# Order of the three passes in split products, and a norm handed over before a mixer, in a two-layer kernel on one core

## The chip, the cores and the metric

The kernel runs on one core of a Trainium2 chip. The metric is the device time of one execution in microseconds; lower is better. The core has five engines with a queue each: TensorE (PE in the profile), which multiplies and transposes, VectorE (DVE), ScalarE (ACT), GpSimd (POOL) and SyncE (SP), which here issues nearly all DMA transfers.

## The reference

Four batches of 512 rows of 256 values pass through two layers. Each layer normalizes its input, computes a mixed part `s` and a gate `g`, and adds their product:

```
xn = layernorm(x)
s  = mix(xn)                      # layer 0: linear map, RMS norm, plus xn; layer 1: attention, plus xn
g  = silu(W2 · fwht(silu(W1·xn) * (W3·xn)))
x  = x + s * g
```

In layer 0 the recurrence starts from zero and runs one step, so its mix is one 256 x 256 matrix, followed by an RMS norm. `fwht` is a Walsh-Hadamard transform over the 1024 hidden values. In layer 1 the mix is a causal attention with one head over 512 positions. All is in 32-bit floating point.

## The kernel before

**Split products.** Nearly every operand is kept as two tensors of the type `fp32r`: `hi`, a cast made by ACT, and `lo`, the rest, made by DVE as source minus `hi` (`split`, line 59). A product `l · r` is then three passes that add up in one PSUM bank: hi·hi, hi·lo and lo·hi. `mm3` (line 80) issues them for a list of terms, as a rule two, for the two halves of the 256 input values: first hi·hi of all terms, then for each term `l[0]·r[1]` (upper part of the stationary operand, lower part of the moving one) and `l[1]·r[0]`. Those who call `mm3` are the gate and up products of layer 0 (line 510), the mixer (717), the folded matrices (208 and 235), and in the attention `tq` (782), `v` (791), `sc` (807) and `pv` (858). The products of the hidden values (`down`, lines 469 and 573) and the gate products of layer 1 (`ffn_s`, line 556) write their three passes out themselves.

**Layer 0.** `ffn` (line 461) goes through a batch in eight chunks `c` of 128 hidden values. For each it makes two products, `gu0` and `gu1`, of twelve passes in all, then on ACT the silu, on DVE the product `h`, and the split of `h` into `hh` and `hl`. `down` of a chunk runs one chunk later. The weights come in four quarters, two chunks each; `split_w13` (line 118) makes their two parts in batch 0. Beside the chunks runs a list of tasks, generators that `Beside` (line 872) steps through, a step or so per slot, two slots a chunk. For each batch the list is built in the loop at line 993: in batch 0 the preparation of weights, `mixer(0)` and `norm(0, 1)`; in the later ones the gate of the batch before (`gate_all`), `mixer(b)`, `norm(0, b + 1)`, and preparations for layer 1 (`prep_w2`, `prep_second`, `prep_s`).

`norm(0, b)` (line 426) makes DVE's statistics, POOL's power -0.5, DVE's scaling, eight transposes on PE, and the split of the transposed input `xT` (`xt` in the profile). `mixer(b)` (line 708) makes 24 products of 256 columns in two halves, copies them out (`osb`), squares and sums them on ACT, takes the power on POOL, scales `osb` and adds it to `xn` on DVE.

**What sets the order.** In layer 0 the order in which each engine's instructions stand is chosen when the kernel is built: a scheduler lays them out by its own model of time, from the dependencies and the order in which the code hands them over, with a few ties (`after`). In the queue of an engine that order is then fixed. From line 1065 on, in layer 1, the products are tied to each other in the order of the code. The tags of PSUM that matter here are `gu` (three banks, the gate and up products), `ms` (three, transposes, mixer and most others) and `dn` (two, the sums over the chunks).

Of the kernel before, what the change touches and what calls it, by code (L numbers as in the profile page):

```python
# [35 lines left out]
def kernel(ctx: ExitStack, tc: tile.TileContext, a: dict, out: bass.AP):  # L36
# [40 lines left out]
    def transpose(*args):  # L77
        return in_line(nc.tensor.transpose, *args)

    def mm3(o, terms):  # L80

        seq = [(l[0], r[0]) for l, r in terms]
        for l, r in terms:
            seq += [(l[0], r[1]), (l[1], r[0])]
        for n, (l, r) in enumerate(seq):
            ins = matmul(o, l, r, start=n == 0, stop=n == len(seq) - 1)
        return ins
# [128 lines left out]
    def sl(i):  # L216
        return slice(i * P, (i + 1) * P)
# [80 lines left out]
    ALLS = slice(0, S)  # L298
    ALLD = slice(0, D)
# [161 lines left out]
    def ffn(name, xT, w13, w2, slot, defer=1, spare=(), parts=1, behind=False, tail=()):  # L461

        w2h, w2l = w2
        dn, outs, firsts = [], [], {}

        def down(c, hh, hl, tiles=range(NT)):
            if not dn:  # L470
                dn.extend(psum(f"{name}dn{i}", [P, 2, D], tag="dn", bufs=2) for i in range(2))
                outs.extend(dn[t // 2][:, t % 2, :] for t in range(NT))
            for t in tiles:
                o = outs[t]
                for n, (l, r) in enumerate(((hh, w2h), (hh, w2l), (hl, w2h))):
                    first = c == 0 and n == 0
                    stop = c == NH - 1 and n == 2

                    def one(start):
                        return matmul(  # L480
                            o, l[:, sl(t)], r[:, c, :], start=start, stop=stop, skip_group_check=True
                        )

                    if first and t % 2 == 1:
                        with tc.issue_after(firsts[t // 2].ins):
                            ins = one(False)
                    elif first:
                        ins = firsts[t // 2] = one(True)  # L490
                    else:
                        ins = one(False)
            return ins

        queue, gates, late = [], [], []
        for c in range(NH):
            with after(gates[-2] if behind and c >= 2 else None):
                wh, wl = w13(c // 2)
            gu = []
            for j in range(2):  # L500

                o = psum(f"{name}gu{c}_{j}", [P, S], **(DN[0] if behind and c == 1 else GU))
                cols = slice((c % 2) * D + j * P, (c % 2) * D + (j + 1) * P)
                gu.append((o, cols))
            for half in range(parts if c == 0 else 1):
                n = S // (parts if c == 0 else 1)
                ts_ = slice(half * n, (half + 1) * n)
                if parts == 1 or c:
                    for o, cols in gu:
                        last_up = mm3(o[:, ts_], k_pairs((wh, wl), cols, xT, ts_))  # L510
                    continue

                for n, (w, x) in enumerate(((wh, xT[0]), (wl, xT[0]), (wh, xT[1]))):
                    for o, cols in gu:
                        for k in range(2):
                            last_up = matmul(
                                o[:, ts_], w[:, k, cols], x[:, k, ts_],
                                start=n + k == 0, stop=n + k == 3,
                            )
            gu = [o for o, _ in gu]  # L520
            h = hid(f"{name}h{c}")
            first["silu"] = nc.scalar.activation(h, gu[0], AF.Silu)
            gates.append(nc.vector.tensor_tensor(h, h, gu[1], ALU.mult))  # L523
            first["gate"] = gates[-1]
            if c < len(spare):
                hh, hl = spare[c]
            else:
                hh = hid(f"{name}hh{c}", F32R)
                hl = hid(f"{name}hl{c}", F32R)
            if c < len(spare):  # L530
                nc.scalar.copy(hh, h)
                late.append((hl, h, hh))
            else:
                split(h, hh, hl)
            for _ in range(2 if c >= NH - 2 else 0):
                if late:
                    lo_, h_, hi_ = late.pop(0)
                    with after(gates[-1]):
                        nc.vector.tensor_tensor(lo_, h_, hi_.bitcast(F32), ALU.subtract)
            queue.append((c, hh, hl))  # L540
            ups = last_up if behind else None
            with after(gates[-1] if behind else None), after(ups):
                slot(2 * c)
            if len(queue) > defer:
                down(*queue.pop(0))
            with after(gates[-1] if behind else None), after(ups):
                slot(2 * c + 1)
        line["fixed"] = bool(tail)
        line["last"] = last_up
        for what in tail:  # L550
            what()
        for q in queue:
            down(*q)
        return dn
# [153 lines left out]
    def mixer(b):  # L708

        xn, xT, m = xns[0, b], xTs[0, b], first["m"]  # L710
        osb = t4(f"osb{b}", [P, NT, D])
        r = small(f"ssr{b}")
        junk = t2(f"junk{b}", [P, D])
        for i in range(2):
            o = psum(f"o0_{b}_{i}", [P, 2, D])
            for j in range(2):
                mm3(o[:, j, :], k_pairs(xT, sl(2 * i + j), m, ALLD))
            nc.scalar.copy(osb[:, 2 * i : 2 * i + 2, :], o)
            for t in (2 * i, 2 * i + 1):
                nc.scalar.activation(junk, osb[:, t, :], AF.Square, accum_out=r[:, t : t + 1])  # L720
            yield
        nc.vector.tensor_scalar(r, r, 1.0 / D, RMS_EPS, ALU.mult, ALU.add)
        nc.gpsimd.tensor_tensor(r, r, mhalf, ALU.pow)
        for t in range(NT):
            nc.vector.scalar_tensor_tensor(
                osb[:, t, :], osb[:, t, :], r[:, t : t + 1], nwb, ALU.mult, ALU.mult
            )
        nc.vector.tensor_tensor(xn, xn, osb, ALU.add)
        yield

    class Attention:
# [45 lines left out]
        def tq(self, j):  # L777
            b = self.b
            if j == 0:
                self.tqs = t4(f"tqh{b}", [P, 2, S], F32R), t4(f"tql{b}", [P, 2, S], F32R)  # L780
            o = psum(f"tq{b}_{j}", [P, S])
            mm3(o, k_pairs(first["wqk"], sl(j), self.xg, ALLS))
            split(o, self.tqs[0][:, j, :], self.tqs[1][:, j, :])

        def v(self, i, j):
# [207 lines left out]
    for b in range(B):  # L993
        tasks = []
        if b == 0:
            prep = prep_first()
            next(prep)
            tasks.append((prep, 12))
        if b:
            tasks.append((call(gate_all, f"g0_{b - 1}", dn, xns[0, b - 1], xs[b - 1]), 1))  # L1000
        tasks.append((mixer(b), MIXER))
        if b + 1 < B:
            if b:
                load_x(b + 1)
            if b == 2:
                tasks.append((prep_s(0), 4))
            tasks.append((norm(0, b + 1), NORM))
        if b == 0:
            early = w2_tile("early0"), w2_tile("early1")
            spare = [  # L1010
                [early[i][:, 2 * c : 2 * c + 2, :].rearrange("p a d -> p (a d)") for i in range(2)]
                for c in range(NH // 2)
            ]
        if b == 1:
            raw2_1 = load_w2(1)
            w2_1 = w2_tiles(1)
            tasks.append((prep_w2(1, raw2_1, w2_1, t4), W2P))
            tasks.append((prep_second(), 5))
        if b == 2:
            tasks += [(prep_s(1), 4), (norm(1, 0), NORM), (prep_s(2), 4)]  # L1020
        if b == 3:
            atts = [Attention(0)]
            at = atts[0]
            parts = run(at.xt_half, 0), run(at.xt_half, 1), at.xt, at.scaled, at.split_sums
            tasks += [(call(f), 1) for f in parts]
            norms = {1: norm(1, 1)}
            tasks.append((prep_s(3), 4))
        bg = Beside(*tasks)
        if b == 0:
            dn = ffn("f0_0", xTs[0, 0], w13, w2, bg.slot, NH, spare, parts=2, behind=True)  # L1030
        else:
            tail = [run(atts[0].tq, j) for j in range(2)] if b + 1 == B else []
            dn = ffn(f"f0_{b}", xTs[0, b], w13, w2, bg.slot, tail=tail)
        bg.finish()
# [148 lines left out]
```

## Time and profile before

| what | us |
|---|---|
| median of 3 runs (lowest, highest) | 361.06 (361.01, 361.54) |
| the profiled execution | 361.18 |
| its span, first to last instruction | 359.4 |
| PE busy | 352.8 |
| DVE busy | 287.5 |
| ACT busy | 197.9 |
| POOL busy | 20.8 |

All lines of the profile come from one execution. A row of its timeline has the start, the time, the engine, the line of the kernel, the operation and what it writes and reads (output<-inputs), the shapes and the count; a bracket at its end tells how long the engine was idle before and what ended the wait. Numbers of buffers and of chunks are left out in such names, so `f_2hl` is the lower part of the hidden values of any chunk, and the number tells the batch. `PEld` is the loading of a product's stationary operand. Products are pipelined: a row's time overlaps the next one's, so the pace is read from the starts. A line of `L70` is that of the helper through which all products pass.

### The profile page before, as it was taken

How to read it: one execution, taken by the hardware profiler on the slowest of the kernel's cores; microseconds unless marked ns; L12 is line 12 of the kernel's file. 1: busy time of each engine (PE TensorE's matmuls, PEld its weight loads, DVE VectorE, ACT ScalarE, POOL GpSimd, SP SyncE). 2: the span in 40 equal slices, each digit the busy share in tenths (PEclk: the TensorE clock that was granted, in tenths of full speed). 3: DMA queues.
4: the chain of work that ended last, by engine and by line, in shares of the span. 5: the costliest groups of instructions: out<-in, count | busy, mean ns of one | idle time of the engine just before them, and what ended most of it. 6: DMA issues, size and time to landing. Idle time of an engine off the chain costs nothing.

```text
span 359.4 us, 6279 instructions
## 1 busy us (share of the span) xinstructions
PE 352.8 (98%) x2477; PEld 327.2 (91%) x2477; DVE 287.5 (80%) x597; ACT 197.9 (55%) x373; POOL 20.8 (6%) x22
## 2 busy tenths in 40 slices
PE   8999999999999999999999999999999999999995
PEld 6878988888988898888999999999999999999995
DVE  6899658998579938998987957989679897568646
ACT  4666156265463425664477655576555676556443
POOL 2000110300020110100100001100011000000000
PEclk9999999999999999999999999999999999999999
DMA  7935000301044317656256136652554645345401
GB/s 237 339 102 192 2 1 2 114 3 60 0 168 172 132 44 249 243 181 191 90 216 253 58 148 207 226 208 95 204 193 162 214 169 204 128 159 196 191 2 58
DMA packets 16285, 52.25 MB, mean 145 GB/s; under 512 B 1633, under 2 KB 7937, under 8 KB 16257
## 3 DMA queue, kind: packets, MB, share of 16 engines
q1 hardware_dynamic: 15968, 51.60, 40.6%
q8 instruction: 19, 0.31, 0.4%
q10 hardware_dynamic: 288, 0.26, 0.2%
q14 instruction: 10, 0.07, 0.1%
HBM read 42.40 MB, written 9.45 MB: 144 GB/s over the span
## 4 chain that ended last, share of the span: by engine, by line
PE 85%; DVE 12%; ACT 1%; DMA 1%; POOL 1%; issue 0%; DVEq 0%
PE f_0gu L70 6%; PE f_1gu L70 6%; PE f_2gu L70 6%; PE f_3gu L70 6%; PE f_3dn L70 6%; PE f_2dn L70 6%; PE f_0dn L70 5%; PE f_1dn L70 5%; PE pv L70 4%; PE o L70 3%; PE tq L70 3%; PE v L70 2%; PE sc L70 2%; PE w2ps L70 1%; PE pt L70 1%; DVE neg L814 1%
## 5 line engine op out<-in xcount | busy, mean ns | idle before, releaser
L70 PE MATMUL f_1gu<-xt,w 128*128 128x512 f32 x96 | 24.9, 396 | 0.3 <-ACT xt L61 0.3
L70 PE MATMUL f_3gu<-xt,w 128*128 128x512 f32 x96 | 25.0, 396 | 0.0
L70 PE MATMUL f_2gu<-xt,w 128*128 128x512 f32 x96 | 24.8, 395 | 0.0
L70 PE MATMUL f_0gu<-xt,w 128*128 128x512 f32 (+1 forms) x108 | 24.3, 378 | 0.0
L70 PEld LDWEIGHTS f_0gu<-xt,w 128*128 128x128 f32 x108 | 18.4, 188 | 4.6 <-issue 1.0
L70 PEld LDWEIGHTS f_1gu<-xt,w 128*128 128x128 f32 x96 | 17.0, 188 | 3.7 <-ACT xt L61 0.5
L70 PEld LDWEIGHTS f_2gu<-xt,w 128*128 128x128 f32 x96 | 17.0, 188 | 3.0
L70 PEld LDWEIGHTS f_3gu<-xt,w 128*128 128x128 f32 x96 | 17.0, 188 | 2.9
L61 ACT CAST f_2hh<-f_2h 128x512 fp32r<-128x512 f32 x16 | 9.9, 622 | 15.6 <-DVE f_2h L523 12.5
L70 PE MATMUL f_3dn<-w2l,f_3hh 128*128 128x256 f32 x64 | 17.7, 281 | 0.0
L70 PE MATMUL f_3dn<-w2h,f_3hh 128*128 128x256 f32 x64 | 17.7, 281 | 0.0
L70 PE MATMUL f_1dn<-w2l,f_1hh 128*128 128x256 f32 x64 | 17.7, 281 | 0.0
L70 PE MATMUL f_2dn<-w2h,f_2hh 128*128 128x256 f32 x64 | 17.7, 282 | 0.0
L70 PE MATMUL f_1dn<-w2h,f_1hh 128*128 128x256 f32 x64 | 17.6, 280 | 0.0
L70 PE MATMUL f_2dn<-w2l,f_2hh 128*128 128x256 f32 x64 | 17.6, 280 | 0.0
L70 PE MATMUL f_3dn<-w2h,f_3hl 128*128 128x256 f32 x64 | 17.0, 281 | 0.0
L70 PE MATMUL f_1dn<-w2h,f_1hl 128*128 128x256 f32 x64 | 17.0, 281 | 0.0
L70 PE MATMUL f_2dn<-w2h,f_2hl 128*128 128x256 f32 x64 | 16.7, 281 | 0.0
L61 ACT CAST f_3hh<-f_3h 128x512 fp32r<-128x512 f32 (+1 forms) x17 | 10.0, 595 | 10.1 <-DVE f_3h L523 6.0
L61 ACT CAST f_1hh<-f_1h 128x512 fp32r<-128x512 f32 x16 | 9.9, 622 | 9.7 <-DVE f_1h L523 6.6
L62 DVE TENSOR_TENSOR f_2hl<-f_2h,f_2hh 128x512 fp32r<-128x512 f32 x16 | 10.9, 680 | 3.9 <-ACT f_2hh L61 3.8
L70 PE MATMUL f_0dn<-w2h,f_0hl 128*128 128x256 f32 x48 | 13.7, 284 | 0.1
(487 smaller groups left out, 1146.1 us busy)
## 6 DMA issues: line engine op xcount, KB each, us to landing
sw<-s SPq DMA_DIRECT2D x32, 896.0 KB, 5.4
s<-sp SPq DMA_DIRECT2D x8, 512.0 KB, 4.0
s<-sp SPq DMA_DIRECT2D x8, 384.0 KB, 2.8
w2raw<-in_w SPq DMA_DIRECT2D x4, 512.0 KB, 5.1
sraw<-in_w SPq DMA_DIRECT2D x4, 512.0 KB, 3.3
mrb<-there SPq DMA_DIRECT2D x4, 512.0 KB, 3.7
w13raw<-in_w SPq DMA_DIRECT2D x3, 512.0 KB, 6.1
x<-in_x SPq DMA_DIRECT2D x3, 512.0 KB, 3.5
```

The source lines that it names most:

```text
L61: h = nc.scalar.copy(hi, src)
L62: return h, engine.tensor_tensor(lo, src, hi.bitcast(F32), ALU.subtract)
L70: ins = call(*args, **kwargs)
L814: nc.vector.reduce_max(self.neg[:, t : t + 1], self.scs[t][:, : (t + 1) * P], AX.X, negate=True)
```

## The change

`mm3` gets a parameter `late`, the side of the product whose lower part comes last. It no longer goes term by term: after the hi·hi passes of all terms come the passes with the lower part of one side, for all terms, then those with the lower part of the other. With `late=0`, the default, the lower part of the stationary operand `l` is last, with `late=1` that of the moving operand `r`. The gate and up products of layer 0, the mixer and `tq` pass `late=1`; their moving operands are the transposed input, the mixer's matrix and `xg`. The second edit is in the list of tasks of batch 0 alone: `norm(0, 1)` is handed over ahead of `mixer(0)`, where it came after it.

```diff
-    def mm3(o, terms):
+    def mm3(o, terms, late=0):
 
         seq = [(l[0], r[0]) for l, r in terms]
-        for l, r in terms:
-            seq += [(l[0], r[1]), (l[1], r[0])]
+        for side in (1 - late, late):
+            seq += [(l[1 - side], r[side]) for l, r in terms]
         for n, (l, r) in enumerate(seq):
             ins = matmul(o, l, r, start=n == 0, stop=n == len(seq) - 1)
...
-                        last_up = mm3(o[:, ts_], k_pairs((wh, wl), cols, xT, ts_))
+                        last_up = mm3(o[:, ts_], k_pairs((wh, wl), cols, xT, ts_), late=1)
...
-                mm3(o[:, j, :], k_pairs(xT, sl(2 * i + j), m, ALLD))
+                mm3(o[:, j, :], k_pairs(xT, sl(2 * i + j), m, ALLD), late=1)
...
-            mm3(o, k_pairs(first["wqk"], sl(j), self.xg, ALLS))
+            mm3(o, k_pairs(first["wqk"], sl(j), self.xg, ALLS), late=1)
...
-        tasks.append((mixer(b), MIXER))
+        if b:
+            tasks.append((mixer(b), MIXER))
         if b + 1 < B:
             if b:
                 load_x(b + 1)
             if b == 2:
                 tasks.append((prep_s(0), 4))
             tasks.append((norm(0, b + 1), NORM))
+        if b == 0:
+            tasks.append((mixer(b), MIXER))
```

The scheduler makes a new order of layer 0 from this, on every engine.

## The prediction

> **What bounds the kernel now.** I read the page first: TensorE (PE) is busy for 98% of the span, VectorE (DVE) for 80%.
>
> ```profile
> PE 352.8 (98%) x2477; PEld 327.2 (91%) x2477; DVE 287.5 (80%) x597; ACT 197.9 (55%) x373; POOL 20.8 (6%) x22
> PE   8999999999999999999999999999999999999995
> DVE  6899658998579938998987957989679897568646
> ```
>
> So only three things can move the time: PE work (the change neither adds nor removes a product), the head before the first real product, and gaps in the PE stream. A busy PE hides gaps, so I took the starts of successive products from the timeline: a 512-column product follows the last one after 0.233 us, a 256-column one after 0.118 (8 in 0.94). Where a start is late, PE waited; after such a wait the next product is some 0.10 late too, which I call the bubble. Before has two gaps that the change can reach. At the border between batches 0 and 1 of layer 0, PE waits for the transposed input of batch 1; the product before it starts at 50.88, so 51.00 was due:
>
> ```profile
> 50.85 1.07 ACT L61 CAST xt<-xt_1tp 128x512 fp32r<-128x512 f32 x2 [0.66 <-PE xt_1tp L70]
> 51.49 0.74 PE L70 MATMUL f_1gu<-xt,w 128*128 128x512 f32 x2 [0.33 <-ACT xt L61]
> ```
>
> In layer 1, `tq` of batch 1 waits for the lower part of `xg` (206.25 was due), and its next start is 0.34 on instead of 0.23:
>
> ```profile
> 205.66 0.68 DVE L62 TENSOR_TENSOR xgl<-xg,xgh 128x512 fp32r<-128x512 f32 x1
> 206.39 0.19 PEld L70 LDWEIGHTS tq<-xgl,wqkh 128*128 128x128 f32 x1 [0.42 <-DVE xgl L62]
> 206.39 0.50 PE L70 MATMUL tq<-xgl,wqkh 128*128 128x512 f32 x1
> ```
>
> Between 52 and 180 us PE has no gap over 0.1: every lower part comes in time, but by how much is the question. These rows of DVE say it:
>
> ```profile
> 14.10 1.22 DVE L62 TENSOR_TENSOR w<-w13raw,w 128x1024 fp32r<-128x1024 f32 x1
> ...
> 106.13 1.67 DVE L725 SCALAR_TENSOR_TENSOR osb<-osb,ssr,nwb 128x256 f32<-128x256 f32 x4 [0.30 <-POOL ssr L723]
> 107.72 0.68 DVE L523 TENSOR_TENSOR f_2h<-f_2h,f_2gu 128x512 f32<-128x512 f32 x1
> ...
> 112.22 0.66 DVE L62 TENSOR_TENSOR f_2hl<-f_2h,f_2hh 128x512 fp32r<-128x512 f32 x1
> 112.80 0.42 DVE L329 TENSOR_TENSOR ssum<-sraw 128x256 f32<-128x256 f32 x1
> ...
> 114.36 0.92 DVE L62 TENSOR_TENSOR sp<-sraw,sp 128x768 fp32r<-128x768 f32 x1
> ```
>
> The first makes the lower part of weight quarter 1, ready at 15.32. `f_2hl` of chunk 2 is ready at 112.88 and read by PE at 113.85, a cover of 0.97.
>
> [...]
>
> **The change part by part.** The order of instructions in the two built kernels shows more than the diff: the scheduler moved much of layer 0. All sums are against the profiled execution (361.18, span 359.4); the median of the runs is 0.12 less.
>
> 1. *tq, lower `xg` last.* Its two products on `xgl` become the fifth and sixth. The first starts at 205.32, the fifth is due at 206.25 and needs half 0 (long made); the sixth is due at 206.49, half 1 is there at 206.39. Gain 0.14 + 0.10 = 0.24.
>
> 2. *Gate and up products, lower `xT` last.* For batch 0 it is the weights that are late, not `xT`. Chunks 2 and 3 start at 13.56. Before, nine products (hi·hi twice and hi·xT-lower, three groups) stood ahead of the first that reads the lower weights, due at 13.56 + 9 × 0.233 = 15.65. Now six do: 14.96. The split ends at 15.32, and PE sees an end about 0.05 later (206.34 to 206.39 above): wait 0.41, bubble 0.10, cost 0.51. ACT and DVE stand in the same order up to there, so nothing moves the split. Quarters 2 and 3 are split earlier against their use, free.
>
> 3. *Mixer and the other three-pass products.* Same count, same pace; before has no gap in them. 0.
>
> 4. *Norm of batch 1 ahead of mixer 0.* The eight transposes of `xt_1` now stand about 50 products before the end of batch 0, at some 42.8 (with part 2's delay). Their input: DVE's four stats (1.32) go ahead of `wgl`, the scaling ends near 41.1, in time. ACT's two casts end near 45. The gap at 51.00 goes: gain 0.49 + 0.10 = 0.59. Mixer 0's own products move behind, which delays what hangs on them: ACT's squares, POOL's power, DVE's `osb`, `xn`, the gate.
>
> 5. *What is late next, batch 1.* Batch 1 starts at 51.00 + 0.51 = 51.5, as before. The last mixer product has 19 small ones between it and that start: 51.49 - 20 × 0.118 = 49.13. From there as before: 0.32 to ACT's copy, then copy 0.48, two squares at 0.54 (49.45 to 51.0), 1.29 to `osb` (48.04 to 49.33), 1.71 to `xn`, 1.14 for it: DVE is free at 55.1, where before it did `xn` at 51.04. From then on it is never idle until `hl` of chunk 2: 17 operations of 512 columns at 0.60, two of 1024 at 1.14, stats 1.32, `osb` 1.58, small ones 0.48, together 15.9. It starts at 71.0, is seen at 71.73. PE wants it after 60 × 0.233 + 52 × 0.118 = 20.12: 71.61. Wait 0.12, bubble 0.10: 0.22.
>
> 6. *Batch 2.* PE's products up to the last of mixer 2 are the same set, so it starts at 99.28 - 0.10 (bubble gone) + 0.22 = 99.40. Then ACT: 0.32 + 0.48 + 2 × 0.54 + cast of `sraw` 0.83 = 102.11. DVE, now behind that cast: split 0.87, last `ssum` 0.42, ACT's cast 1.05, DVE's big split from 104.5. Then 1.14, `hl` 0.60, `osb` 1.58, `h` 0.60, eight stats 2.63, `xn` 1.13, and, newly ahead of `hl` of chunk 2, two `ssum` 0.67, a 768-column split 0.87 and two more aggregates 0.17 (two were there: 0.17). It starts at 114.06, is seen at 114.79. PE wants it at 113.85 - 0.10 + 0.22 = 113.97. Wait 0.82, bubble 0.10: 0.92. On SP's queue the load of `sraw` now stands behind a store that waits for ACT's cast, and ACT's cast of `sraw` ahead of `hh`: SP issues it near 104.9 instead of 104.57, it lands near 110.8 (before: 110.46), `hh` is ready at 112.2, wanted at 112.11. That 0.1 and a gate slot freed late lie inside the wait for `hl`.
>
> 7. *Covers that shrink elsewhere.* DVE enters layer 1 later against PE, and several lower parts have 0.2 to 0.4 of cover where they had more. No row prices this. Below: 0, if covers hold; a gain is excluded, as the other gaps of layer 1 stand at products that the change doesn't touch. Above: 0.4, four slips of one bubble. I take 0.15.
>
> Sum: -0.24 + 0.51 - 0.59 + 0.22 + 0.92 + 0.15 = +0.97, so 362.1 for the profiled execution and 362.0 for the median.
>
> **The rivals.** *Not slower: DVE makes `hl` of chunk 2 in time in batches 1 and 2.* Place: the two splits of parts 5 and 6. It decides if DVE is 0.1 earlier in batch 1 and 0.8 earlier in batch 2, as when `sraw`'s cast doesn't hold DVE. Then -0.24 + 0.51 - 0.59 = -0.32: 360.7. For: before has an idle DVE at 100.5 and 105.8. Against: what stands ahead in the queue is fixed by the order, and each length is measured. *Faster* takes more: the lower weights in time as well, all gains alone, -0.83: 360.2. *Half of it:* the batch 2 wait is 0.4, batch 1 none: 361.2 to 361.5. *A transfer becomes the bound:* `sraw` lands 1 us later (it shares the queue with stores), `hh`, then the splits, slip with it: 362.9. *The change does nothing:* the new order is there in the built kernel, so PE must differ; I give that none.
>
> **How the numbers follow.** 0.2% is 0.72 us, about what a measurement of this kernel can tell from no change. All three waits as summed (361.7 to 362.5): 60%. Late transfer: 10%. Half: 17%. Splits in time: 9%. Faster: 4%. Slower begins at 361.78, so the first case gives it nine parts in ten, 0.54, the second all of its 0.10: 0.64. Same takes the rest of the first, the half and the splits in time: 0.32. Faster: 0.04. The range leaves out the last two cases below and the end of the late transfer above: 361.1 to 362.8; the likeliest case alone is 361.7 to 362.5.
>
> **What would show it.** PE starts `f_0gu` on the lower weights at 15.4 with DVE's split as releaser (part 2); no wait at `f_1gu` near 51.5 (4); `tq` of batch 1 at an even 0.233 (1); `f_1dn` waits for `f_1hl` near 71.6 (5), `f_2dn` for `f_2hl` near 114 by about 0.8 (6). It is wrong if the last two waits are missing, or if layer 1, whose order in PE is written out, shows new gaps.

## The result, and the profile after

The kernel became slower: 362.75 us (median of 6 runs, 362.66 to 363.0) against 361.13 (361.01 to 361.62), a ratio of 1.0041 with a 95% interval of 1.0032 to 1.0051, or +1.62 us. The forecast was 362.0, its range 361.1 to 362.8. The profiled execution took 362.67 us, its span is 360.9 (before: 361.18 and 359.4).

The busy times of the page say nothing of this. PE has the same work and the same time as before:

```profile
PE 352.9 (98%) x2477; PEld 326.9 (91%) x2477; DVE 287.3 (80%) x597; ACT 197.1 (55%) x373; POOL 18.9 (5%) x22
```

The table of waits on PE does (columns: who waited for whom; us in all, times, longest):

```profile
PE f_3dn L70 <- DVE f_3hl L62: 0.7, 1, 0.7
PE f_2dn L70 <- DVE f_2hl L62: 0.5, 1, 0.5
...
PE f_0gu L70 <- DVE w L62: 0.2, 1, 0.2
```

The wait for the transposed input at the border is gone from it, and three waits for lower parts made by DVE are new. The table counts idle time between modelled ends, which is less than what a late start costs (0.7 for 0.94 at `f_3hl`), so I take the starts again, from PE's timeline of the kernel after:

```profile
15.21 0.96 PE L70 MATMUL f_0gu<-xt,w 128*128 128x512 f32 x3 [0.25 <-DVE w L62]
...
51.25 0.28 PE L70 MATMUL f_0dn<-w2h,f_0hl 128*128 128x256 f32 x1
51.37 0.86 PE L70 MATMUL f_1gu<-xt,w 128*128 128x512 f32 x3
...
71.69 0.39 PE L70 MATMUL f_1dn<-w2h,f_1hl 128*128 128x256 f32 x1
...
114.54 0.39 PE L70 MATMUL f_2dn<-w2h,f_2hl 128*128 128x256 f32 x1 [0.48 <-DVE f_2hl L62]
...
171.82 0.39 PE L70 MATMUL f_3dn<-w2h,f_3hl 128*128 128x256 f32 x1 [0.68 <-DVE f_3hl L62]
```

`f_1gu` starts 0.12 after the last product of batch 0: the border has no wait. Against the pace the others start late by 0.41 (lower weights), 0.22 (`f_1hl`), 0.64 (`f_2hl`) and 0.84 (`f_3hl`), and each loses 0.10 more at the next product: 0.51, 0.32, 0.75 and 0.94. PE did not go past the late product: those behind the one at 171.82, on an `f_3hh` that PE had read at 170.75, start at 172.05 and 172.16. With -0.60 at the border and -0.24 at `tq` the sum is +1.68. This execution started its first real product at 7.63 instead of 7.83, which leaves +1.5, the difference of the spans.

The last of these waits, at `f_3hl`, was not in the forecast. Its cause is seen three steps back. SP's timeline of the kernel after, at the end of layer 0:

```profile
149.51 9.18 SPq L350 DMA_DIRECT2D sw<-s  x2
158.79 0.38 SPq L325 DMA_DIRECT2D sraw<-in_w  x1
```

and of the kernel before:

```profile
148.68 0.32 SPq L349 DMA_DIRECT2D sw<-s  x1
149.05 0.42 SPq L324 DMA_DIRECT2D sraw<-in_w  x1
```

The second load of `sw` goes to a place of the tag `w13` that PE still reads, so SP stands at it. The waits on SP between 140 and 170 us, kernel after:

```profile
SPq L350 <- PE f_3gu L70: 13.2, 2, 8.5
```

Before, the load of `sraw` (batch 3's weights for layer 1) was issued ahead of it; after, behind it, 9.7 us later. DVE's timeline of the kernel after shows what follows:

```profile
164.50 0.43 DVE L330 TENSOR_TENSOR ssum<-sraw 128x256 f32<-128x256 f32 x1 [1.75 <-DMA sraw<-in_w]
...
169.23 1.21 DVE L62 TENSOR_TENSOR sp<-ssum,sp 128x1024 fp32r<-128x1024 f32 x1
...
171.11 0.66 DVE L62 TENSOR_TENSOR f_3hl<-f_3h,f_3hh 128x512 fp32r<-128x512 f32 x1
```

and the same three of the kernel before:

```profile
158.94 0.41 DVE L329 TENSOR_TENSOR ssum<-sraw 128x256 f32<-128x256 f32 x1
...
164.34 1.23 DVE L62 TENSOR_TENSOR sp<-ssum,sp 128x1024 fp32r<-128x1024 f32 x1 [0.27 <-ACT sp L61]
...
168.69 0.66 DVE L62 TENSOR_TENSOR f_3hl<-f_3h,f_3hh 128x512 fp32r<-128x512 f32 x1
```

DVE idles 1.75 us for the load and then does late what before was long done; `f_3hl` of the last chunk comes 2.4 us later. The chain of work that ended last runs through the transfer (start, us, what):

```profile
158.79 5.58 DMA sraw<-in_w
166.53 0.87 DVE sp L62
168.00 1.31 DVE ln_1st L272 x4
171.82 1.44 PE f_3dn L70 x10
```

### The profile page after: what moved, and what is told of

Same layout as the page of the kernel before. It is cut to its first block, busy times and chain, and to the rows that moved or that the text cites. A ratio compares the mean times of both kernels' runs of the same rounds, so it can differ in the third digit from the quotient of the medians.

```text
span 360.9 us, 6279 instructions
## 1 busy us (share of the span) xinstructions
PE 352.9 (98%) x2477; PEld 326.9 (91%) x2477; DVE 287.3 (80%) x597; ACT 197.1 (55%) x373; POOL 18.9 (5%) x22
## 4 chain that ended last, share of the span: by engine, by line
PE 70%; DVE 22%; ACT 2%; DMA 2%; issue 2%; POOL 1%; DVEq 0%; SPq 0%
PE f_0gu L70 5%; PE f_2dn L70 5%; PE f_3dn L70 5%; PE f_3gu L70 5%; PE f_0dn L70 5%; PE pv L70 4%; PE f_1dn L70 4%; PE f_2gu L70 3%; PE o L70 2%; PE v L70 2%; PE f_1gu L70 2%; PE tq L70 2%; PE sc L70 2%; DMA sraw<-in_w 2%; DVE osb L726 1%
## 5 line engine op out<-in xcount | busy, mean ns | idle before, releaser
L70 PE MATMUL f_0dn<-w2l,f_0hh 128*128 128x256 f32 x48 | 13.5, 282 | 0.0
```

The source lines that it names most:

```text
L70: ins = call(*args, **kwargs)
```

## The experiments

Ten kernels, one of them run twice, and the kernel after once more. All PE starts are read as above. The table has what each wait cost PE in the profiled execution, late start and bubble together, and the median beside that of the kernel before in the same comparison.

| kernel | us (before) | lower weights | `f_0dn` | border | `f_1hl` | `f_2hl` | `f_3hl` | `tq` |
|---|---|---|---|---|---|---|---|---|
| before | 361.13 | - | - | 0.60 | - | - | - | 0.24 |
| after | 362.75 (361.13) | 0.51 | - | - | 0.32 | 0.75 | 0.94 | - |
| after, again | 362.83 (361.26) | 0.52 | - | - | 0.34 | 0.75 | 0.92 | - |
| e1: passes alone | 361.27 (361.22) | 0.52 | - | 0.36 | - | - | - | - |
| e2: norm alone | 362.62 (361.22) | - | 0.57 | - | 0.33 | 0.75 | 0.86 | 0.26 |
| e3: after, weights last | 362.89 (361.22) | - | 0.37 | - | 0.34 | 0.75 | 0.75 | - |
| e3 again | 362.83 (361.26) | - | 0.39 | - | 0.34 | 0.75 | 0.58 | - |
| e4: `tq` alone | 361.05 (361.30) | - | - | 0.60 | - | - | - | - |
| e5: after, `sraw` first | 361.92 (361.22) | 0.52 | - | - | 0.33 | 0.75 | - | - |
| e6: after, split on GpSimd | 361.26 (361.30) | 0.57 | - | - | 0.33 | - | - | - |
| e7: norm inside mixer | 361.20 (361.30) | - | - | - | - | 0.75 | - | - |
| e8: e7, split on GpSimd | 360.34 (361.30) | - | - | - | - | - | - | - |
| e9: e8, new passes | 360.87 (361.26) | 0.52 | - | - | - | - | - | - |
| e10: e7 with a tie | 360.32 (361.28) | - | - | - | - | - | - | - |

### Each edit alone

Theory W of the expectations is the forecast's mechanism with the fourth wait added; its rivals put the loss on the passes, or on both edits together. e1 has the new `mm3` with its `late=1`, and the list of tasks as in the kernel before. e2 has only this:

```diff
-        tasks.append((mixer(b), MIXER))
+        if b:
+            tasks.append((mixer(b), MIXER))
...
             tasks.append((norm(0, b + 1), NORM))
+        if b == 0:
+            tasks.append((mixer(b), MIXER))
```

> The new order of the passes alone, the tasks of batch 0 as in the kernel before. Theory W (each late lower part costs its own wait, and the moved norm is what makes the hidden lower parts late): PE waits for the lower weights of quarter 1 in batch 0 (+0.51) and no longer at tq of batch 1 (-0.24); the border wait of batch 1 shrinks, because PE arrives there 0.5 later while the chain to the transposed input is only partly held back (-0.1 to -0.5); none of the three new waits at f_1hl, f_2hl and f_3hl. Sum -0.2 to +0.2 against before: 361.0 to 361.4. Rival P (the new order of the passes is what slows the kernel as a whole): 362.4 to 362.8, with the waits at f_2hl and f_3hl in place.

> The norm of batch 1 ahead of mixer 0 alone, the passes in the old order. Theory W: the waits at f_1hl (+0.32), f_2hl (+0.75) and f_3hl (+0.94) are all there, the border wait is gone (-0.60), the lower weights come in time, tq of batch 1 keeps its wait: +1.4, 362.4 to 362.7. Rival P (the passes cause it): the three waits are missing, 360.5 to 361.2. Rival J (it takes both edits together to make the last wait): +0.5, 361.5 to 361.8.

The passes alone: 361.27, a ratio of 1.0002 (0.9994 to 1.001). The wait of 0.52 for the weights is there, and is paid by `tq` (-0.24) and by the border, where PE arrives later and waits 0.36 instead of 0.60. The norm alone: 362.62, a ratio of 1.0041 (1.0029 to 1.0054). So the moved norm alone costs 1.4 us, of the 1.6 for both edits. (The waits of its profiled execution sum to 1.9; at 363.0 it was the longest of the five.) The three waits of the hidden values come with it, as the waits on PE in e2 show:

```profile
PE f_3dn L70 <- DVE f_3hl L62: 0.6, 1, 0.6
PE f_2dn L70 <- DVE f_2hl L62: 0.5, 1, 0.5
...
PE f_0dn L70 <- DVE early L539: 0.3, 1, 0.3
```

The last line was not expected: with the norm early and the weights in time, PE comes to the lower hidden values `early` of batch 0 before DVE has made them; the product starts at 39.54. Rivals P and J fall.

### The lower weights

e3 is the kernel after with the weights' lower part last in batch 0, where `behind` is true:

```diff
-    last_up = mm3(o[:, ts_], k_pairs((wh, wl), cols, xT, ts_), late=1)
+    last_up = mm3(o[:, ts_], k_pairs((wh, wl), cols, xT, ts_), late=int(not behind))
```

> The kernel after, but with the lower weights instead of the lower input as the last passes of gate and up in batch 0. Theory W: the wait of 0.41 + 0.10 for the lower weights goes, the rest stays; PE then reaches the later splits 0.5 earlier, so a part comes back as a new or longer wait before batch 1 (0 to 0.4): 362.2 to 362.6. Rival C (the wait for the weights only moved PE behind other waits, so it costs nothing of its own): 362.6 to 362.9, the waits at f_1hl or f_2hl longer by as much.

It gave 362.89, rival C's number: the wait for the weights went and nothing was won. But `f_1hl` and `f_2hl` do not wait longer, as C had it. A second run, with the kernel after beside it:

> The kernel with the lower weights last in batch 0 once more, beside the kernel after in the same call, since its first run was 0.14 above the kernel after although its gaps sum to 0.34 less, and its first product of batch 0 started at 8.21, that of the kernel after at 7.63. Theory F (the first product's start differs from execution to execution and hid a gain of 0.3): 0.2 to 0.4 under the kernel after in the medians. Rival B (VectorE in batch 0 keeps its own time, so PE loses at f_0dn in exchange for the weights what it won): the same as the kernel after within 0.15, and the wait at f_0dn near 39.7 is longer by as much as the first product starts earlier.

> The kernel after, to compare in one call with the kernel with the lower weights last in batch 0: 362.7 to 362.9. Theory F: the first product's start is another than 7.63 and the span follows it. Rival B: the product on the lower weights starts at 15.2 as before whatever the first product does.

The medians were the same again, 362.83 and 362.83, so theory F misses in the medians. In the profiles 0.37 and 0.39 of the 0.51 come back in batch 0, both times at a product of `f_0dn` behind DVE's `early`. PE's and DVE's rows in the first profile of e3:

```profile
39.42 0.28 PE L70 MATMUL f_0dn<-w2l,early 128*128 128x256 f32 x1
39.81 0.39 PE L70 MATMUL f_0dn<-w2h,early 128*128 128x256 f32 x1
```

```profile
39.07 1.29 DVE L540 TENSOR_TENSOR early<-f_0h,early 128x512 fp32r<-128x512 f32 x2
```

Each of the two on DVE takes 0.68, so the first ends at 39.75; PE's product was due at 39.54. PE's rows in the second profile:

```profile
38.87 0.28 PE L70 MATMUL f_0dn<-w2l,early 128*128 128x256 f32 x1
39.28 0.50 PE L70 MATMUL f_0dn<-w2h,early 128*128 128x256 f32 x2
```

Rival B's prediction, that this wait grows by as much as the first product is earlier, is wrong: that start was 8.21 in one and 7.56 in the other. Nor does the product on the lower weights keep its time: in the second profile of the kernel after it starts at 15.38 instead of 15.21, with the first product at 7.79 instead of 7.63. From the first product to the end of the span e3 takes 352.9 and 353.0, the kernel after 353.3 both times; so the profiles show 0.3 to 0.4 won, since `f_3hl` waits less, and the medians of five runs show none. The five runs of e3's second series go from 362.32 to 363.46, wider than any other kernel's here. The two profiled executions of e3, 362.92 and 362.32, differ by 0.60, and their first products by 0.65, so between these two it is the start that differs; whether it spreads the other runs too stays open.

Where nothing waits afterwards, the same order of passes does cost. e9 is e8 (below) with the new passes everywhere, and nothing else:

> The kernel with the norm between the halves of mixer 0, the split on GpSimd and sraw first on SP, now with the new order of passes everywhere. Only the wait for the lower weights of quarter 1 in batch 0 can be new against the run with the old passes. Theory A (a wait costs its 0.51 in full where no later wait was there to take it up, and none was seen in batch 0 of that run): 360.8 to 361.0 if that run stands at 360.34. Rival C (the wait for the weights costs nothing, as the run with the weights last seemed to say): 360.2 to 360.5.

360.87 against 360.34: 0.53 for a wait of 0.41 + 0.10. PE's timeline in e9:

```profile
15.13 0.73 PE L70 MATMUL f_0gu<-xt,w 128*128 128x512 f32 x2 [0.25 <-DVE w L62]
```

So the price of part 2 was right by itself, but in the kernel after it mostly stands in for a wait that would follow.

### tq alone

Only `tq` gets `late=1`, all else is the kernel before.

> The kernel before with one edit: tq alone takes its passes in the new order, the lower xg last. Theory W: the products of layer 0 stand as in the kernel before, the wait of 0.14 + 0.10 at tq of batch 1 goes, nothing takes its place: -0.24 against before, 360.9 to 361.1 beside a before of 361.2. Rival H (the cover is taken back by the next wait for DVE, at f1_1gu near 235): no difference, 361.2.

361.05 against 361.30, a ratio of 0.9993 (0.9985 to 1.0001). The median and the profile agree with -0.24, the interval just includes no change. No later wait is longer (0.27 near 235 and 0.26 near 282; in the kernel before 0.27 and 0.28), which speaks against rival H.

### sraw first

```diff
-        nc.sync.dma_start(raw, a["w13_1"][q])
+        first[f"sraw{q}"] = nc.sync.dma_start(raw, a["w13_1"][q])
...
-        for i in range(2):
-            nc.sync.dma_start(parts[i].bitcast(F32), sdram[q][i])
+        with after(first["sraw3"] if n == 1 else None):
+            for i in range(2):
+                nc.sync.dma_start(parts[i].bitcast(F32), sdram[q][i])
```

> The kernel after, with one tie: the second load of sw stands behind the load of batch 3's sraw on SP's queue, as it stood in the kernel before. Theory Q (SP's queue causes the last wait): sraw lands before 157, ssum starts by 160, f_3hl of chunk 7 is ready before 170.5 and the wait of 0.84 + 0.11 goes: 361.6 to 362.0. Rival V (DVE's own queue in batch 3 is late whatever SP does): f_3hl still comes at 171.5 or later, 362.4 to 362.8.

361.92, and no wait at `f_3hl`: 0.70 over the kernel before of its comparison, where the kernel after is 1.62 over, so 0.9 less. SP's rows of e5:

```profile
150.14 0.38 SPq L325 DMA_DIRECT2D sraw<-in_w  x1
158.60 0.32 SPq L351 DMA_DIRECT2D sw<-s  x1
```

The load goes out at 150.14, and `f_3hl` of the last chunk starts at 168.49 instead of 171.11. One detail of theory Q was wrong: DVE's first `ssum` starts at 162.89, not by 160. Rival V falls.

### What stands ahead of f_2hl

e6 has one edit to the kernel after: for batch 0's weights of layer 1 the subtraction of the first split goes to GpSimd.

```diff
-            split(src[:, :n, :], *parts)
+            split(src[:, :n, :], *parts, engine=nc.gpsimd if q == 0 and not at else nc.vector)
```

> The kernel after, but the lower part of batch 0's weights for layer 1 (the 128x768 split of sraw, 0.92 on DVE, which stands ahead of the hidden values of chunk 2 in batch 2) is made on GpSimd; SP's order at the end of layer 0 comes out as in the run with the tie. Theory D (DVE's queue is what makes f_2hl late, so whatever leaves it brings f_2hl forward by its own length): no wait at f_2hl of chunk 2, no wait at f_3hl: 361.0 to 361.4, 0.7 under the run with the tie. Rival S (f_2hl is late through the load of sraw and ACT's cast ahead of hh, not through DVE): f_2hl waits by 0.5 or more still: 361.7 to 362.0. Rival G (GpSimd and VectorE hold each other up): VectorE's operations beside the split take longer, a wait of 0.3 or more stays, 361.5 or more.

361.26, 0.66 under e5; the wait at `f_2hl` is gone. The number is theory D's, but the reason I gave is not what the trace shows. The split that went to GpSimd stands at 102, ten us ahead, and DVE only idled there 0.87 for PE. What stood directly ahead of `f_2hl` of chunk 2 in the kernel after belongs to batch 1's weights:

```profile
112.01 0.42 DVE L330 TENSOR_TENSOR ssum<-sraw 128x256 f32<-128x256 f32 x1
112.34 0.41 DVE L331 TENSOR_TENSOR ssum<-sraw 128x256 f32<-128x256 f32 x1
...
112.83 0.92 DVE L62 TENSOR_TENSOR sp<-sraw,sp 128x768 fp32r<-128x768 f32 x1
...
113.83 0.65 DVE L62 TENSOR_TENSOR f_2hl<-f_2h,f_2hh 128x512 fp32r<-128x512 f32 x1
```

In e6 the scheduler, planning anew, had put these three behind `f_2hl`:

```profile
112.31 0.66 DVE L62 TENSOR_TENSOR f_2hl<-f_2h,f_2hh 128x512 fp32r<-128x512 f32 x1
...
112.98 0.39 DVE L330 TENSOR_TENSOR ssum<-sraw 128x256 f32<-128x256 f32 x1
113.29 0.42 DVE L331 TENSOR_TENSOR ssum<-sraw 128x256 f32<-128x256 f32 x1
...
114.45 0.92 DVE L62 TENSOR_TENSOR sp<-sraw,sp 128x768 fp32r<-128x768 f32 x1
```

It also put the load of `sraw` in batch 3 ahead of the second load of `sw` (149.45 and 156.98 on SP), without e5's tie, so `f_3hl` is in time as well. e10 tests the order on DVE alone, without GpSimd. It starts from e7, in which the steps of norm (`n`) and mixer (`m`) of batch 0 are interleaved as `mnnmmn`, only `tq` has the new passes, and `sraw` is first on SP:

```diff
+    def in_turn(order, **steps):
+        for which in order:
+            next(steps[which])
+            yield
...
+            tasks.append((in_turn("mnnmmn", m=mixer(b), n=norm(0, b + 1)), MIXER + NORM))
```

> Norm of batch 1 handed over between the two halves of mixer 0 (mixer half 0, statistics and first four transposes, mixer half 1, mixer's end, last four transposes), passes as in before except for tq in the new order, sraw of batch 3 ahead of the second load of sw. Theory D: the border wait is gone (-0.60), tq (-0.24), mixer 0 ends soon enough that f_1hl of chunk 2 comes in time; f_2hl still waits (+0.75 to +0.95), f_3hl does not: -0.1 to +0.1 against before, 361.1 to 361.3. Rival N (handing the norm over early delays f_1hl wherever in the mixer it stands): f_1hl waits by 0.3 or more, 361.4 to 361.7.

e7 gave 361.20 beside 361.30. The border and `f_1hl` are in time, `f_2hl` is late by the same 0.75 as in the kernel after. So rival N falls: `f_1hl` was late because all of mixer 0 stood behind the norm (DVE starts `xn` of mixer 0 at 51.04 in the kernel before, 54.03 in the kernel after, 52.79 in e7). e8 is e7 with e6's line:

> The kernel of the run with the norm between the halves of the mixer, and the 128x768 split of batch 0's weights for layer 1 on GpSimd as well. Theory D: all gains of the change stay and none of its waits: -0.60 and -0.24 against before, 360.3 to 360.5 beside a before of 361.2. Rival G (GpSimd and VectorE hold each other up, or its slower split comes late): a new wait in batch 2 of 0.3 or more, 360.7 to 361.2.

360.34, a ratio of 0.9975 (0.9966 to 0.9984), without any wait over 0.12 in layer 0 that the kernel before didn't have. Then e10, e7 with this instead of GpSimd:

```diff
-        nc.vector.tensor_tensor(s1, a21, a22, ALU.add)
-        nc.vector.tensor_tensor(s3, a11, a21, ALU.subtract)
+        with after(first["lo"] if q == 1 else None):
+            nc.vector.tensor_tensor(s1, a21, a22, ALU.add)
+        with after(first["lo"] if q == 1 else None):
+            nc.vector.tensor_tensor(s3, a11, a21, ALU.subtract)
...
-            split(src[:, :n, :], *parts)
+            with after(first["lo"] if q == 1 and not at else None):
+                split(src[:, :n, :], *parts)
...
-                split(h, hh, hl)
+                lo = split(h, hh, hl)[1]
+                if c == 2:
+                    first["lo"] = lo
```

> The kernel with the norm between the halves of mixer 0, nothing on GpSimd, but with a tie: the first two sums and the 128x768 split of batch 1's weights for layer 1 (0.42 + 0.42 + 0.92 on DVE; these, and not batch 0's split that went to GpSimd, are what stands ahead of f_2hl of chunk 2) come behind f_2hl of chunk 2. Theory O (the place of these three in DVE's queue is the whole cause of the wait, and the run on GpSimd lost it only because the three fell behind): f_2hl is made about 1.5 earlier, no wait in batch 2, 360.3 to 360.5 beside 361.2 to 361.3 before, as with GpSimd. Rival L (DVE needs the 0.92 that GpSimd took over, or its work is late further on): a wait of 0.3 or more at a later f_2hl or f_3hl, 360.7 to 361.2.

360.32, a ratio of 0.9973 (0.9963 to 0.9983): the same as with GpSimd. DVE's and PE's rows of e10:

```profile
111.56 0.67 DVE L62 TENSOR_TENSOR f_2hl<-f_2h,f_2hh 128x512 fp32r<-128x512 f32 x1
112.13 0.42 DVE L335 TENSOR_TENSOR ssum<-sraw 128x256 f32<-128x256 f32 x1
...
113.69 0.93 DVE L62 TENSOR_TENSOR sp<-sraw,sp 128x768 fp32r<-128x768 f32 x1
```

```profile
111.91 1.55 PE L70 MATMUL f_2gu<-xt,w 128*128 128x512 f32 x6
113.30 0.28 PE L70 MATMUL f_2dn<-w2h,f_2hl 128*128 128x256 f32 x1
```

`f_2hl` now stands ahead of the three, ends at 112.23, and PE starts on it at the pace (6 x 0.233 after 111.91). In e7, with the three ahead of it, it starts at 113.25 instead of 111.56. Theory O holds: the order in DVE's queue was the cause, DVE's load was not. e8 and e10 beat both kernels of the change, by 0.96 us against before.

## Why the prediction was right or wrong

**1, tq: right.** -0.24 in the profile of after and in e4.

**2, lower weights: the size right, its worth only in part.** 0.51 was forecast, 0.51 measured, at 15.21. What I left out is that the waits are not independent: e3 takes this one away and gains nothing in the median, e9 adds it to a kernel without other waits and loses all of it.

**3, the other three-pass products: right**, 0: the kernel after and e1 have no new gap at them.

**4, the border: right**, -0.60 for -0.59, and e7 keeps it.

**5, f_1hl: right**, 0.32 for 0.22. It is mixer 0 behind the norm, as the step had it: e7 puts half of the mixer ahead and the wait is gone.

**6, f_2hl: right in mechanism**, 0.75 for 0.92. The step named two `ssum` and the 768-column split ahead of `f_2hl`, and e10 shows that these are the cause. The first term of the wait, 0.82, measured 0.64: counted from the first real product, PE came 0.1 later than reckoned, through part 5, and the split ended a little earlier.

**7, the covers elsewhere: wrong.** This step failed. It allowed 0 to 0.4, as slips of a bubble each, and took 0.15; there was one full wait of 0.94 in batch 3. "DVE enters layer 1 later" was not its cause, and layer 1 itself has no new gap (near 191, 236 and 283 PE starts 0.26, 0.26 and 0.28 late, before the same within 0.01). The cause was the order on SP: I had followed the load of `sraw` past a store in batch 2, but not the load of batch 3, which came behind a load that waits for PE. e5 undoes that one order and gets 0.9 back. With 0.94 for 0.15, and the smaller misses of 5 and 6, +0.97 becomes the measured +1.7.

**The rivals.** "Not slower" needed both splits in time; neither was. "A transfer becomes the bound" had the right kind of event (`sraw` late on SP) in the wrong batch and with the wrong delay; at 10% it was held too low. The sign was right. That the range held the time, by 0.05, was luck: the largest single wait was not in the sum, the likeliest case alone (361.7 to 362.5) missed the time, and the two ends of part 7 were set without looking at all the transfers that the new order moves.

## What to carry to other kernels

When a new order comes out of a scheduler, go through every queue of it, the DMA queues too, and look for a transfer or a split that now stands behind an instruction which waits for another engine: one such place (0.9 us here) outweighed both intended gains (0.84). Waits of a stream that is busy throughout don't add up simply; taking one away may only bring the stream to the next late operand (0.51 taken away in e3, 0.37 and 0.39 back at `f_0dn`), so the price of a wait is tested in a kernel without the others. And a late operand can be cured by order alone: here a tie that puts three operations behind it did as much as moving work to another engine (360.32 and 360.34).

## What the runs showed of the hardware

The first real product starts at another time in each execution, also of one kernel: 7.63 and 7.79 for the kernel after, 8.21 and 7.56 for e3. At first PE makes a 512-column product in 0.43 us. The step to 0.233, a factor of 1.8, came near 4.5 us of the span in the kernel after and near 5.0 in the kernel before. In e3 the two products of `warm` at 7.02 still took 1.00 together; in the kernel after the two at 6.62 took 0.72. So the moment of the step differs between executions; what sets it was not shown. Nor does the step alone set the first product's start: in e1 the first eleven products of `warm` took 5.06 together, as in e3, against 4.42 in the kernel before, but its first real product started at 7.89, only 0.06 after that of the kernel before (7.83). So profiles of one execution each are better compared from the first product on.

GpSimd took 1.85 us for the split of 128x768 that takes DVE 0.92 to 0.96, and one of DVE's operations took longer beside it. GpSimd's and DVE's rows in e6:

```profile
102.31 1.85 POOL L62 TENSOR_TENSOR sp<-sraw,sp 128x768 fp32r<-128x768 f32 x1 [29.45 <-ACT sp L61]
```

```profile
102.83 0.69 DVE L524 TENSOR_TENSOR f_2h<-f_2h,f_2gu 128x512 f32<-128x512 f32 x1 [0.87 <-PE f_2gu L70]
103.44 0.75 DVE L723 TENSOR_SCALAR ssr<-ssr 128x4 f32<-128x4 f32 x1
```

The `TENSOR_SCALAR` of four columns takes 0.16 in e10, without GpSimd; here it ends 0.03 after GpSimd's split. In e8 the same operation took 0.74 and ended 0.02 after the split. The `TENSOR_TENSOR` on `f_2gu`, beside the same split, keeps its 0.69 (0.68 in e10). Why the one took longer and the other did not, no run here shows. It cost PE nothing: e8, with the split on GpSimd, takes 360.34, and e10, without, 360.32.
